# Leftover scatters of a graph kernel placed behind the next group's gathers, and the list sums' first step and pace changed

## The chip, the cores and the metric

The kernel runs on one core of one Trainium2 chip. A core has a matrix engine (TensorE, PE in the profile), a vector engine (VectorE, DVE), a scalar engine (ScalarE, ACT), a general engine (GpSimd, POOL) and a queue engine (SyncE, SP). POOL and SP issue most of the DMAs here; DMAs with an index per row (gathers and scatters) are issued by POOL. The metric is the device time of one launch in microseconds; the time before is the median of three runs.

## The reference

Four graph layers run one after the other on x of 16 x 1024 x 256 (16 graphs, 1024 nodes, 256 features) with one adjacency matrix adj of 1024 x 1024. A little over 1.5% of adj is nonzero, the diagonal included, so a row has some 17 neighbours.

```python
# layer 0: a score for each pair of nodes, wanted only where adj is not zero
pre_u = einsum('bud,dk->buk', h, W1[:d]);  pre_v = einsum('bvd,dk->bvk', h, W1[d:])
hidden = relu(pre_u[:, :, None, :] + pre_v[:, None, :, :] + b1)
S = sigmoid(einsum('buvk,ko->buvo', hidden, W2)[..., 0] + b2)
a = einsum('buv,bud->bvd', S * adj, h)
m = einsum('uv,bud->bvd', adj, h) * h
z = beta1 * h + beta2 * (a @ Wa + ba) + beta3 * (m @ Wm + bm)
# layer 1: neighbours' sum, projected
x = z + relu(einsum('ij,bjd->bid', adj, z) @ W.T + b)
# layers 2 and 3: attention with a rank-one logit and a dense bias
feats = x @ W1.T;  f = feats @ W2 + b2
coefs = softmax(leaky_relu(f[:, :, None] + f[:, None, :]) + adj)
x = coefs @ feats + bias2 + x
```

## The kernel before

**Lists in place of the dense pair tensor.** The scores of layer 0 are computed only for pairs that adj has. For each row the kernel finds up to 32 neighbours (SLOTS); the first 16 (FIRST) stand in the row's own list, the others in quads (QUAD, four slots) of extra rows, packed into 6 extra tiles of 128 rows (XT). The 16 graphs are treated in 4 groups (NGR) of 4 graphs (GB). For a group there are 8 tiles of 128 rows with 16 steps each and 6 extra tiles with 4 steps each: 152 score steps a group, 608 in all.

**A score step** (`score_steps`, L704 to L839) takes one slot of one tile for the four graphs of the group. POOL gathers 128 rows of v (`fetch`, L857, the indirect DMA at L695) into a tile z of 128 x 1024, four steps ahead (LEAD), with six z tiles. DVE adds u (L805), then takes relu times the score weights (L807), ACT sums each graph's 256 columns (four activations, L811). At a tile's last step the sigmoid is made (L820 to L824) and its 16 or 4 scatters are put on the list `waiting`; each writes the four graphs' scores of one slot to a dense array in HBM (`scatter`, L700). In the following steps one scatter is written per step, or two on odd steps while more than four wait (L786), each after that step's gather in POOL's queue. At the end of a group all that is left in `waiting` is written at once (L831 to L833) and the group is entered in `finished`. An engine takes the instructions of its queue in order, so a gather that is queued behind such a run of scatters waits for it.

**The order of the stages.** In a first part (`score_free`) PE computes the products that need no scores, for all 16 graphs. Then follow for each group: `with_edges`, which loads the dense scores (`load_gd`) and multiplies them with the projected features; and two times `pair_layers`, which takes two graphs through layer 1 (`layer_one`, that is `projected` and `neighbours`) and layers 2 and 3 (`front`, `scales`, `sums`). `sums` makes the attention weights m on DVE (L1036), and PE multiplies them.

**The interleaving is written out by hand.** Each of these stages is a generator that yields planned PE microseconds. `Side.along` counts them times a rate (RATE: 0.26 in the first part, 0.255 later) and advances the score steps by one for each whole unit. `paced` ties such an instruction to a PE product a few back, so that it doesn't run ahead. Score steps, stage work and list steps thus share the engines' queues in the order in which they were written. Before a group's `with_edges`, steps are forced until that group is in `finished` (L1303).

**The list sums.** The last group has no scores beside it. There the layer-1 neighbour sum of its second pair is split: nodes 768 to 1023 by products with adj (`neighbours`), nodes 0 to 767 (FAR = 6 tiles) by list: `by_lists` (L1139) gathers rows of y and adds them, weighted, into `msg`: 24 steps for the extra tiles, whose results are stored to part_d from SP, then 96 for the tiles' own slots, then 24 that add the extra rows. A tile's first step (k = 0, L1174) writes the tile on ACT; the other steps add on DVE (L1176, L1172). `far_ahead` places these 144 steps beside the first pair's layers, with a rate of 0.88 for the first 68 planned units (the first pair's `layer_one`) and 0.58 after that (L1293). At the end of layer one `onto` takes relu of the sums on ACT (L1116) and adds them to z on DVE (L1117); the fronts' products need that z. The second pair's stages begin with `from_lists`, which transposes msg on PE (L1193).

Of the kernel before, what the change touches and what calls it, by code (L numbers as in the profile page):

```python
# [12 lines left out]
AF = mybir.ActivationFunctionType  # L13
ALU = mybir.AluOpType
# [24 lines left out]
def after(tc, ins, others, kind, why):  # L39
    dep = mybir.DependencyInfo(kind, mybir.DependencyReason.DATA)  # L40
    for o in others:
        tc.add_manual_dep(ins.ins, o.ins.name, dep, reason=why)
# [23 lines left out]
def gnn_stack_kernel(  # L66
# [27 lines left out]
    nc = tc.nc  # L94
# [23 lines left out]
    def paced(ins, back=6):  # L118


        if recent:
            after(tc, ins, [recent[max(0, len(recent) - back)]], mybir.DependencyClass.Sync, "keeps pace")
        return ins
# [122 lines left out]
    NGR = B // GB  # L246
# [117 lines left out]
    with ExitStack() as stack:  # L364
# [126 lines left out]
        to = prep1.tile([P, NF], F32, name="to")  # L491
# [183 lines left out]
    with tc.If(listed > 0) as arm:  # L675
        with ExitStack() as stack:
# [13 lines left out]
            put = [Scatters(tc, f"scores {g}") for g in range(NGR)]  # L690
            finished = []
# [12 lines left out]
            def score_steps(pool):  # L704
# [8 lines left out]
                us, zt, ss = {}, {}, {}  # L713
# [62 lines left out]
                def unpack(got):  # L776
                    paced(nc.vector.tensor_copy(x_node, got[:, :, : 1 + QUAD]))
                    nc.vector.tensor_copy(x_a, got[:, :, 1 + QUAD : 1 + 2 * QUAD])
                    nc.vector.tensor_copy(x_at, got[:, :, 1 + 2 * QUAD : 1 + 3 * QUAD])

                moved, got, arrive = None, None, 0
                later = mybir.DependencyClass.NoSync
                for n, (g, t, k) in enumerate(todo):
                    if n + LEAD < len(todo):
                        last = fetch(us, zt, *todo[n + LEAD])
                    for _ in range(0 if n < HOLD else 2 if n % 2 and len(waiting) > 4 else 1):  # L786
                        if waiting:
                            group, *what = waiting.pop(0)
                            ins = scatter(*what)
                            group.add(ins)  # L790
                            after(tc, ins, [last], later, "behind the gather")
                    if moving:
                        group, *what = moving.pop(0)
                        ins = scatter(*what)
                        group.add(ins)
                        after(tc, ins, [last], later, "behind the gather")
                        arrive = n + 12
                    slots, _, at, av = lists(t)
                    z, u = zt.pop((g, t, k)), us[g, t]
                    if k == 0:  # L800
                        ss[t] = small.tile([P, FIRST, GB], F32, tag="s", name="s")
                    s = ss[t]
                    if k == 0 and (g, t) in follows:
                        sources(us, *follows[g, t])
                    paced(nc.vector.tensor_tensor(z, z, u, ALU.add))  # L805
                    zk = z.rearrange("p (c k) -> p c k", k=D)
                    nc.vector.scalar_tensor_tensor(  # L807
                        zk, zk, 0.0, w2r[:, None, :].to_broadcast([P, GB, D]), ALU.max, ALU.mult
                    )
                    for c in range(GB):  # L810
                        nc.scalar.activation(zk[:, c, :], zk[:, c, :], AF.Copy, accum_out=s[:, k, c : c + 1])  # L811
                    if n < NT:
                        search(others, n)
                    if n == NT:
                        places(others)
                    if n == NT + 4:
                        moved = to_extra_rows()
                    if k == slots - 1:
                        sv = s[:, :slots, :].rearrange("p s c -> p (s c)")
                        nc.scalar.activation(sv, sv, AF.Exp, bias=nb2, scale=-1.0)  # L820
                        nc.vector.tensor_scalar(sv, sv, 1.0, None, ALU.add)
                        nc.vector.reciprocal(sv, sv)
                        gt = small.tile([P, FIRST, GB], F32, tag="g", name="gt")
                        nc.vector.tensor_tensor(  # L824
                            gt[:, :slots, :], s[:, :slots, :],
                            av[:, :slots].unsqueeze(2).to_broadcast([P, slots, GB]), ALU.mult,
                        )
                        for j in range(slots):
                            waiting.append((put[g], dense[g % BUFS], at[:, j : j + 1], gt[:, j, :]))
                        if t == last_of[g]:  # L830
                            for group, *what in waiting:  # L831
                                group.add(scatter(*what))
                            waiting.clear()  # L833
                            finished.append(g)
                    if moved and not moving and n == arrive:
                        got = from_extra_rows(moved)
                    if got is not None and n == arrive + 24:
                        unpack(got)
                    yield  # L839

            def lists(t):
                if t < NT:
                    return FIRST, slot_v[:, t, :], slot_at[:, t, :], slot_a[:, t, :]
                return QUAD, x_node[:, t - NT, 1:], x_at[:, t - NT, :], x_a[:, t - NT, :]
# [294 lines left out]
            def by_lists(msg):  # L1139

                spares = [gd_pool.tile([P, QN, GB], F32, tag="gd", name="msg") for _ in range(4)]
                halves = [
                    t.rearrange("p n i -> p (n i)")[:, k * 2 * D : (k + 1) * 2 * D] for t in spares for k in range(2)
                ]
                msg.extend(halves[:FAR])
                part = halves[FAR:]
                nc.gpsimd.memset(part[0], 0.0)
                nc.sync.dma_start(part_d[XT * P :, :], part[0])

                nc.vector.tensor_scalar(to_u, to_u, float(XT * P), None, ALU.min)  # L1150
                todo = [(NT + i, k) for i in range(XT) for k in range(QUAD)]
                todo += [(t, k) for t in range(FAR) for k in range(FIRST)]
                todo += [(t, FIRST + q) for t in range(FAR) for q in range(NG)]
                got = {}

                def fetch_row(t, k):
                    z = got[t, k] = slot_pool.tile([P, GB * D], F32, tag="z", name="z")[:, : 2 * D]
                    if t < NT and k >= FIRST:
                        at = (k - FIRST) * NT + t
                        gather(z, part_d, to_u[:, at : at + 1])  # L1160
                    else:
                        gather(z, y_d, lists(t)[1][:, k : k + 1])

                for step in todo[:LEAD]:
                    fetch_row(*step)
                for n, (t, k) in enumerate(todo):
                    if n + LEAD < len(todo):
                        fetch_row(*todo[n + LEAD])
                    z = got.pop((t, k))
                    to = msg[t] if t < NT else part[t % len(part)]  # L1170
                    if t < NT and k >= FIRST:
                        paced(nc.vector.tensor_tensor(to, to, z, ALU.add))  # L1172
                    elif k == 0:
                        paced(nc.scalar.activation(to, z, AF.Copy, scale=lists(t)[3][:, k : k + 1]))  # L1174
                    else:
                        paced(nc.vector.scalar_tensor_tensor(  # L1176
                            to, z, lists(t)[3][:, k : k + 1], to, ALU.mult, ALU.add
                        ))
                    if t >= NT and k == QUAD - 1:
                        nc.sync.dma_start(part_d[(t - NT) * P : (t - NT + 1) * P, :], to)  # L1180
                    yield
# [100 lines left out]
            def far_ahead(z, main):  # L1282

                both = y_d.rearrange("(t p) (i d) -> p t i d", p=P, i=2)
                y = yield from projected(z, lambda i, ts, y: nc.sync.dma_start(both[:, ts, i, :], y))
                yield from neighbours(y, z, slice(FAR * P, N))
                gone, far = 0.0, Side(by_lists(msg))

                def slots():
                    nonlocal gone  # L1290
                    for us in main:
                        gone += us
                        yield us * (0.88 if gone < 68 else 0.58)  # L1293

                far.along(slots())
                for _ in far.steps:
                    pass
                yield 0
# [147 lines left out]
```

## Time and profile before

| | |
|---|---|
| median of three runs | 3205.61 us (3198.1 to 3207.4) |
| the profiled execution | 3224.95 us |
| its span, first to last instruction | 3223.1 us |
| scatters of scores on POOL (L700) | 512 of 1255 ns and 96 of 1174 ns |
| gathers of v on POOL (L695) | 512 of 1261 ns and 96 of 1285 ns |
| list steps on ACT (L1174) | 12 of 720 ns |
| list steps on DVE (L1176, L1172) | 108 of 751 ns, 24 of 690 ns |
| granted TensorE clock over the span | 0.99 |

How to read it: PE is the busiest engine, and a matmul takes the same time wherever it stands, so the time of a stage is its matmuls plus the pieces in which PE is idle or runs at a reduced clock. A timeline line gives start, duration, engine, source line, operation, output and input, how many instructions are merged in it, and in brackets how long the engine was idle before it and what ended that. Line numbers are those of the kernel; L126 is a helper that issues most products, L695 and L700 are helpers that issue all gathers and scatters, so that the tile names tell which is meant. A windows line gives, for a stretch of the span, its length and then the busy time of PE, of the weight loads, of DVE, ACT and POOL, each with a count, and after them the granted clock, the share of the DMA engines and GB/s.

### The profile page before, as it was taken

The page shows a single profiled execution, that of the slowest core. Times are in us where ns is not written, and L with a number is a line of the kernel's source. Part 1 is how long each engine was busy: PE and PEld are TensorE (multiplying, and loading weights), DVE is VectorE, ACT ScalarE, POOL GpSimd, SP SyncE. Part 2 cuts the span into 40 slices and gives each one's busy share as a digit, 9 for nine tenths or more (in the row PEclk, how much of TensorE's full clock was granted, in tenths as well). Part 3 has the DMA queues.
Part 4 walks back from the last instruction along what each step waited for, and adds up shares of the span by engine and source line. Part 5 has one row for each costly group of instructions (what it writes and reads, how often), then busy time and mean ns, then how long its engine had stood idle before and what let it go on. Part 6 is the DMA issues. An engine that isn't in the chain of part 4 may idle for free. (4 is left out here: it accounts for less than half of the span.)

```text
span 3223.1 us, 39246 instructions
## 1 busy us (share of the span) xinstructions
PE 3127.4 (97%) x12122; PEld 2203.7 (68%) x12122; DVE 2349.9 (73%) x3162; ACT 1955.7 (61%) x6524; POOL 1819.4 (56%) x1483
## 2 busy tenths in 40 slices
PE   8899999999999999999999999899999999998999
PEld 5444544545557668678876867777587688857888
DVE  7797767677774789789768978877798891147744
ACT  3245555666668767567977756688676774413342
POOL 1146778676764656657666665556676652076500
PEclk9999999999999999999999999999999999999999
DMA  9899898888889755756876575587657644485600
GB/s 315 292 323 322 267 288 263 265 242 249 271 284 343 211 167 150 229 158 203 300 233 171 158 212 177 161 284 239 187 151 212 181 145 145 131 256 154 156 7 28
DMA packets 281994, 687.48 MB, mean 213 GB/s; under 512 B 45280, under 2 KB 137440, under 8 KB 274608
## 3 DMA queue, kind: packets, MB, share of 16 engines
q0 software_dynamic: 128224, 387.80, 41.6%
q1 hardware_dynamic: 126112, 245.98, 22.2%
q10 hardware_dynamic: 27440, 51.13, 4.2%
q8 instruction: 97, 1.59, 0.2%
q14 instruction: 121, 0.99, 0.1%
HBM read 553.45 MB, written 131.32 MB: 212 GB/s over the span
## 5 line engine op out<-in xcount | busy, mean ns | idle before, releaser
L811 ACT ACTIVATE z<-z 128x256 f32<-128x256 f32 x2432 | 979.8, 407 | 642.3 <-DVE z L807 568.8
L805 DVE TENSOR_TENSOR z<-z,u 128x1024 f32<-128x1024 f32 x608 | 738.9, 1220 | 435.9 <-PE bank L126 291.9
L126 PE MATMUL bank<-feats,m 128*128 128x257 f32 x4096 | 923.3, 383 | 19.0 <-DVE m L1036 17.8
L695 POOL DMA_INDIRECT z<-v_d,slot_v x512 | 645.9, 1261 | 477.1 <-ACT z L811 264.1
L126 PEld LDWEIGHTS bank<-feats,m 128*128 128x128 f32 x4096 | 771.4, 191 | 138.4 <-DVE m L1036 19.8
L700 POOL DMA_INDIRECT dense_d<-gt,slot_at x512 | 642.5, 1255 | 186.8 <-issue 139.5
L807 DVE SCALAR_TENSOR_TENSOR z<-z,w2r 128x1024 f32<-128x1024 f32 x608 | 738.0, 1220 | 9.0
L126 PE MATMUL bank<-gc,hw 128*128 128x256 f32 x2048 | 456.6, 384 | 25.0 <-ACT gc L1064 17.8
L811 ACT ACTIVATION_READ_ACCUMULATOR z<-z 128x1 f32 x2432 | 463.3, 190 | 0.0
L126 PEld LDWEIGHTS bank<-gc,hw 128*128 128x128 f32 x2048 | 388.6, 192 | 92.5 <-ACT gc L1064 25.9
L126 PE MATMUL bank<-adj_sb,h 128*128 128x512 f32 x1024 | 443.0, 592 | 4.0 <-ACT st L322 2.4
L1036 DVE SCALAR_TENSOR_TENSOR m<-rho,tau,adj_sb 128x512 f32<-128x512 f32 x512 | 375.6, 744 | 72.1 <-PE bank L126 68.5
L126 PE MATMUL bank<-adjT_in,y 128*128 128x512 f32 (+1 forms) x960 | 401.2, 578 | 3.9 <-DMA adjT_in<-adjT_d 2.5
L126 PEld LDWEIGHTS bank<-adj_sb,h 128*128 128x128 f32 x1024 | 194.3, 190 | 244.2 <-issue 239.6
L126 PE MATMUL bank<-w,hT 128*128 128x512 f32 (+1 forms) x1024 | 336.2, 489 | 0.0
L126 PEld LDWEIGHTS bank<-adjT_in,y 128*128 128x128 f32 x960 | 181.9, 190 | 218.9 <-issue 204.3
L1064 ACT ACTIVATE gc<-gd 128x1024 f32<-128x1024 f32 x128 | 265.2, 2074 | 94.0 <-PE bank L126 59.1
L126 PEld LDWEIGHTS bank<-w,hT 128*128 128x128 f32 x1024 | 195.7, 192 | 143.0 <-issue 121.0
L126 PE MATMUL bank<-g_wT,z 128*128 128x257 f32 x1024 | 233.7, 383 | 8.2 <-DVE z L1117 8.2
L695 POOL DMA_INDIRECT z<-v_d,x_node x96 | 123.4, 1285 | 176.7 <-ACT z L811 115.7
L126 PEld LDWEIGHTS bank<-g_wT,z 128*128 128x128 f32 x1024 | 193.2, 191 | 39.0 <-DVE z L1117 8.9
L322 ACT ACTIVATE st<-bank 128x512 f32<-128x512 f32 x128 | 75.6, 590 | 104.3 <-PE bank L126 62.5
(161 smaller groups left out, 2403.2 us busy)
## 6 DMA issues: line engine op xcount, KB each, us to landing
gd<-dense_d SPq DMA_DIRECT2D x128, 512.0 KB
dense_d<-zero ACTq DMA_DIRECT2D x64, 512.0 KB
adjT_in<-adjT_d SPq DMA_DIRECT2D x112, 256.0 KB
h<-in_x_dram SPq DMA_DIRECT2D x19, 1024.0 KB
u_d<-st SPq DMA_DIRECT2D x64, 256.0 KB
v_d<-st SPq DMA_DIRECT2D x64, 256.0 KB
hw_d<-st SPq DMA_DIRECT2D x64, 256.0 KB
u<-u_d POOLq DMA_DIRECT2D x32, 512.0 KB
```

The costliest lines, as they stand in the source:

```text
L126: recent.append(nc.tensor.matmul(*args, **kw))
L322: nc.scalar.activation(st[:, c, :2, :], ps.rearrange("p (s k) -> p s k", s=2), AF.Copy)
L695: return nc.gpsimd.indirect_dma_start(out=dst, out_offset=None, in_=src[:], in_offset=bass.IndirectOffsetOnAxis(ap=at, axis=0), **how,)
L700: return nc.gpsimd.indirect_dma_start(out=dst[:], out_offset=bass.IndirectOffsetOnAxis(ap=at, axis=0), in_=src, in_offset=None,)
L805: paced(nc.vector.tensor_tensor(z, z, u, ALU.add))
L807: nc.vector.scalar_tensor_tensor(zk, zk, 0.0, w2r[:, None, :].to_broadcast([P, GB, D]), ALU.max, ALU.mult)
L811: nc.scalar.activation(zk[:, c, :], zk[:, c, :], AF.Copy, accum_out=s[:, k, c : c + 1])
L1036: nc.vector.scalar_tensor_tensor(m, r[:, cols], ta[:, jt : jt + 1], ea[:, jt, cols], ALU.max, ALU.mult)
L1064: paced(nc.scalar.activation(gc, gd.rearrange("p n i -> p i n"), AF.Copy), 16)
```

## The change

At a group's end the group is put on a new list, `ending`, in place of writing all its scatters. They stay in `waiting` and are written by the loop at L786 in the next group's first steps, each behind that step's gather. A helper `done` enters the group in `finished` when none of its scatters waits any more. For the last group the scatters are still written at once. In `by_lists` the first step of a tile is a multiplication on DVE instead of an activation on ACT, and in `far_ahead` the two rates become 0.80 and 0.61.

```diff
+                ending = []
+
+                def done(group):
+                    if ending and put[ending[0]] is group and all(w[0] is not group for w in waiting):
+                        finished.append(ending.pop(0))
...
                             group.add(ins)
                             after(tc, ins, [last], later, "behind the gather")
+                            done(group)
...
                         if t == last_of[g]:
-                            for group, *what in waiting:
+                            ending.append(g)
+                            while waiting and g == NGR - 1:
+                                group, *what = waiting.pop(0)
                                 group.add(scatter(*what))
-                            waiting.clear()
-                            finished.append(g)
+                                done(group)
...
                     elif k == 0:
-                        paced(nc.scalar.activation(to, z, AF.Copy, scale=lists(t)[3][:, k : k + 1]))
+                        paced(nc.vector.tensor_scalar(to, z, lists(t)[3][:, k : k + 1], None, ALU.mult))
...
-                        yield us * (0.88 if gone < 68 else 0.58)
+                        yield us * (0.8 if gone < 68 else 0.61)
```

## The prediction

> **What bounds the kernel now.** I read the page's busy line first, then the windows of 40 us over the whole span to find where TensorE (PE) stands still, then the timelines of the engines at those places, and the chain of waits last.
>
> ```profile
> PE 3127.4 (97%) x12122; PEld 2203.7 (68%) x12122; DVE 2349.9 (73%) x3162; ACT 1955.7 (61%) x6524; POOL 1819.4 (56%) x1483
> ```
>
> PE sets the time; it is idle for only 3223.1 - 3127.4 = 96 us, the start included. An edit pays only where it removes PE idle time (or keeps PE's clock up). Two pieces of that idle time lie where a group's scores end. This is POOL, then DVE, then PE at the end of group 2's scores (steps counted over all groups, so step 456):
>
> ```profile
> 2018.22 1.39 POOL L700 DMA_INDIRECT dense_d<-gt,slot_at  x1 [0.30 <-issue]
> ...
> 2042.14 0.97 POOL L700 DMA_INDIRECT dense_d<-gt,slot_at  x1 [0.30 <-issue]
> 2043.42 0.97 POOL L695 DMA_INDIRECT z<-v_d,slot_v  x1 [0.30 <-issue]
> ```
>
> ```profile
> 2048.03 1.23 DVE L805 TENSOR_TENSOR z<-z,u 128x1024 f32<-128x1024 f32 x1 [8.32 <-DMA z<-v_d,slot_v]
> ```
>
> ```profile
> 2052.43 9.74 PE L126 MATMUL bank<-feats,m 128*128 128x257 f32 x32 [8.19 <-DVE m L1036]
> ```
>
> POOL issues 16 scatters in a row, 24.9 us without a gather (from 2018.2 to 2043.1). Only the gathers fetched ahead are there to live on, so DVE meets a score step whose row isn't there, waits 8.32 us, and the products behind it in DVE's order (m, L1036) starve PE for 8.19 us. The windows show the second half of the price:
>
> ```profile
> 2040.00:2045.00 5.00, 4.24 (x22) 3.49 (x20) 0.00 (x0) 1.46 (x8) 3.78 (x5) 1.00 0.05 10
> 2045.00:2050.00 5.00, 0.00 (x0) 0.00 (x0) 1.97 (x3) 0.00 (x0) 4.09 (x4) 0.74 0.90 277
> 2050.00:2055.00 5.00, 2.57 (x6) 2.11 (x7) 4.36 (x6) 1.71 (x8) 2.29 (x3) 0.50 0.96 322
> 2055.00:2060.00 5.00, 5.00 (x18) 4.15 (x18) 3.77 (x4) 1.42 (x7) 0.18 (x1) 0.74 0.43 135
> ```
>
> The columns are PE, weight loads, DVE, ACT, POOL, then the granted clock: 0.50 after the gap, so matmuls run at half speed until about 2058. Group 1's end is the same picture (scatters from 1381.0 to 1406.0):
>
> ```profile
> 1412.64 6.19 PE L126 MATMUL bank<-feats,m 128*128 128x257 f32 x20 [3.12 <-DVE m L1036]
> ```
>
> The third place is the list sums beside the last group's first pair. The chain of waits, and PE there:
>
> ```profile
> 2884.00 19.65 issue
> 2903.67 5.42 another core or an unknown queue
> 2909.11 0.73 ACT msg L1174
> 2909.86 0.76 DVE msg L1176
> ```
>
> ```profile
> 2912.90 7.86 PE L126 MATMUL bank<-g_wT,z 128*128 128x257 f32 x24 [7.96 <-DVE z L1117]
> ```
>
> ACT sits behind one list step (L1174, k = 0 of list tile 2), DVE's list steps queue behind that, and the layer-one result z (L1116 on ACT, L1117 on DVE) queues behind those. PE needs z and loses 7.96 us, again with the clock at 0.50 afterwards.
>
> **What the Trainium skill says.** (1) "TensorE: Matmul & The Clock Gate", Part 1: after an idle window of about 3.4 us PE gets half its clock until it has been busy for such a window. The trace agrees: 0.50 after all three gaps. (2) "VectorE: DVE Perf Modes", the perf-mode tier table: an fp32 tensor_scalar in SBUF runs two elements a cycle, a two-tensor operation one. It agrees: the tensor_scalar of w by beta2 (L159, 128x512) took 481 ns, the list step of two tensors (L1176, same size) 750 ns. (3) "SBUF — State Buffer", two separate sides: such a two-port DVE operation locks GpSimd out, which then can't write DMA descriptors. No row of this trace isolates that. I use it as a bound: 0.48 us for each.
>
> **The change part by part, against the profiled execution (3224.95 us, span 3223.1).**
>
> *Scatters at a group's end.* 4 + 16 + 16 scatters of groups 0 to 2 leave the burst and go behind the next group's gathers, two on odd and one on even steps while more than four wait: 12 in eight steps, then four more, 12 steps in all. Group 3 keeps its burst (nothing is gathered after it). No instruction is added.
> - Removed at group 2's end: 8.19 us idle, and 32 matmuls in 9.74 us where 64 of the same took 14.04 us just before (0.219 each, 7.0 for 32): 2.7. Together 10.9 us.
> - Removed at group 1's end: 3.12 + 0.64 (L1219, 1419.46), and 20 matmuls in 6.19 for 4.4: 1.8. Together 5.6 us.
> - Group 0's end (four scatters, 758.7 to 763.7): PE stands at 5.00 of 5 in the windows there. 0.
> - What is late next: POOL now issues 2.5 DMAs a step while it drains. A scatter is 1255 ns, a gather 1261, and 0.30 lies between: 2.5 x 1.56 = 3.9 us. A step comes every 1/0.255 = 3.9 units of planned PE time (one sums stage is 14.8 units, 14.04 us in the trace), so POOL just keeps up, with four to six gathers of lead (some 15 us) as cover. Other tiles' ends drain by this same rule, and in the sums stages none of them shows a DVE wait for z over 1.5 us. Bounds: 0 if the lead holds, 5 us if POOL's DMAs take 1.5 + 0.3 us beside a full DVE (4.5 a step, eight steps, 0.6 late each). I take 1.5 us.
> - Does the next stage wait for the late scatters? Steps done by a point are planned units times the rate: 841.4 x 0.26 = 218.8 in the first part, less 8 searches: 210 scores. Group 0's stages (517.4 x 0.255) bring it to 342, group 1's (536.6 x 0.255) to 479. Group 1 is wanted at 342 and is complete at 304 + 12 = 316; group 2 at 479, complete at 456 + 12 = 468. The loop that forces steps never runs; the closest margin is 11 steps, some 43 us. Cost 0. The loads of dense scores on SP are issued after that and see finished scatters.
>
> Sum: -16.5 + 1.5 = -15.
>
> *First list step on DVE.* 12 activations of 0.72 us leave ACT (8.6 us), 12 tensor_scalars of about 0.48 come to DVE (5.8 us). In these windows DVE is busy 20 to 32 of 40 us, so neither is on the path by itself; what matters is that no list step stands in front of L1116 on ACT any more. If the two-port lock hits POOL each time, 12 x 0.48 = 5.8 us of POOL time, half of it in the stretch where POOL is the pacer. I take 0 on PE, since the new pace leaves room there.
>
> *The pace.* Before, 68 x 0.88 = 59.8 list steps are placed ahead of z's last part; after, 68 x 0.80 = 54.4. A list gather holds POOL 0.95 + 0.30 = 1.25 us, 0.80 a microsecond: 0.88 asks for more than POOL can issue, 0.80 about what it can. In the trace, DVE's step 53 ran at 2900.06. With steps 54 to 58 out of the way, z's four relu and add pairs (0.69 each) can run from PE's end of the stage at 2901.5 and z[0] is ready near 2903.6. PE has work of its own until 2904.9, so it doesn't wait. Removed: 7.96 idle, 24 matmuls in 7.86 for 5.2 (2.6), and the two gaps behind it in the same chain (0.33 and 0.50): 11.4 us. The stores of part_d also hold SP's queue: adjT_in loads at 2855.59 and 2860.00 went straight after such stores and PE waited 0.38 and 0.58. At the slower pace a store falls one load later: another 1.0 at most. In the profiled execution I make this -12.
>
> How much of it is in an ordinary run? The profiled execution is 19 us longer than the median of the three runs shown (3205.61), and 5.42 us of this stall ends by nothing that the profile can name: its gather had landed at 2903.65, its matmuls were recorded done. If an ordinary run lacks those 5.4 us, PE waits about 2.5, too short to lose the clock, and 0.8 + 0.7 for the small gaps: 4 us. The median decides, so I take -4 there (bounds 0 and -12).
>
> *The tail.* 213.9 planned units give 144.5 steps before and 143.4 after; there are 144. So one list step is placed after the pair's last work. It is a 0.69 us add, and PE first transposes four other list tiles (16 transposes, 1.75 us). 0 to 1.3; I take 0.5.
>
> Sum against the profile: -15 - 12 + 0.5 = -26.5, 3198. Against the median: -15 - 4 + 0.5 = -18.5, **3187 us**.
>
> **The rivals.**
> - *Forecast (0.53): both stalls go, 3187.* For it: the burst, the late gather, the wait and the half clock stand in one line. Against: DVE is at 38.5 of 40 us in the sums stages, so it has little to catch up with.
> - *POOL's pace takes the place of the burst (0.20).* The stall is spread, PE gets half of it back later: -8 - 3 = -11, 3195. For it: POOL's 3.9 us a step against 3.9 available. Against: 15 us of lead, and the other tiles' ends.
> - *It doesn't show (0.15).* If POOL runs faster outside the profile (a burst of 17 us instead of 25 would end before the lead is gone) there was no stall to remove; the list stall is the profile's: 3203.
> - *Slower (0.12): the list sums bound the last group.* The second part now holds 89 steps where it held 84.6, in the 150 us from 2912 to 3062: 1.69 us a step. POOL needs 1.21 + 0.30 = 1.51 beside a busy DVE. If a step really costs 2.0 (two-port lock, contention for DMAs), the lists end 89 x 0.31 = 28 us late and PE waits at the transposes: 3187 + 28 = 3215. It costs from 1.69 a step on and turns the sign at 1.69 + 18.5/89 = 1.90. Against: gathers in that stretch mostly wait about 0.5 us for DVE, that is, they are paced, not pacing.
>
> **How the numbers follow.** 0.3% is 9.6 us, about what a measurement of this kernel can tell from no change. The forecast's own range is 3175 (both stalls whole, 30 us) to 3195; with the rivals 3174 to 3206 leaves some 2 in 10 out. Faster by over 0.3%: the forecast nearly whole, three quarters of the second case, little of the third: 0.69. Within: 0.19. Slower: 0.12.
>
> **What would show it.** Right: after each group's last score step POOL alternates gathers and scatters; no DVE wait over 3 us for z there, no clock of 0.50; PE runs through from the last adjT_in product to the fronts in group 3, L1116 with no list step before it on ACT. Wrong: a DVE wait for z of several microseconds some ten steps into the next group; a wait of the dense loads on scatters; PE idle before the transposes of msg (L1193); or the profile improving by over 20 us while the median doesn't move.

## The result and the profile after

The changed kernel takes 3181.4 us, the median of six runs (3169.6 to 3185.6), against 3205.8 us for six runs of the kernel before on the same chip: a ratio of 0.9921, 95% interval [0.9902, 0.9941], 24.4 us less. The profiled execution takes 3181.81 us with a span of 3180.1; that of before had 3223.1. So the profiles differ by 43 us and the medians by 24: the profiled execution of before lay 19 us above its median, that of after lies on its median. The forecast was 3187.

The busy line of the page after (line numbers after the change are 7 or 8 higher than before):

```profile
PE 3117.1 (98%) x12122; PEld 2198.4 (69%) x12122; DVE 2354.2 (74%) x3174; ACT 1946.7 (61%) x6512; POOL 1823.1 (57%) x1483
```

The number of matmuls is the same and PE is still the bound, but it is idle for 3180.1 - 3117.1 = 63 us instead of 96, and its busy time fell by 10 us as well: the clock granted to it, averaged over the span, is 0.994 in place of 0.990. DVE has 12 instructions more and ACT 12 fewer.

POOL at the end of group 2's scores, the place where before had 16 scatters in a row (timeline: start, duration, engine, line, operation, output and input, idle before it):

```profile
2002.52 0.96 POOL L695 DMA_INDIRECT z<-v_d,slot_v  x1 [1.04 <-ACT feats L988]
2003.79 1.38 POOL L700 DMA_INDIRECT dense_d<-gt,slot_at  x1 [0.30 <-issue]
...
2008.55 0.97 POOL L700 DMA_INDIRECT dense_d<-gt,slot_at  x1 [0.30 <-DMA z<-v_d,slot_v]
2009.83 0.97 POOL L695 DMA_INDIRECT z<-v_d,slot_v  x1 [0.30 <-issue]
2011.11 1.36 POOL L700 DMA_INDIRECT dense_d<-gt,slot_at  x1 [0.30 <-issue]
2012.77 1.48 POOL L700 DMA_INDIRECT dense_d<-gt,slot_at  x1 [0.31 <-issue]
2014.56 1.49 POOL L695 DMA_INDIRECT z<-v_d,slot_v  x1 [0.30 <-issue]
```

A gather now comes after four scatters, then after one or two. POOL issues without a pause until the last of the 16 at 2044.07. What DVE waited for over this stretch (1990 to 2060 us; total, times, longest), and two of the 5 us windows (PE, weight loads, DVE, ACT, POOL, granted clock):

```profile
DVE z L812 <- PE bank L126: 2.4, 4, 0.8
DVE m L1044 <- PE bank L126: 0.8, 1, 0.8
```

```profile
2035.00:2040.00 5.00, 5.00 (x27) 4.37 (x26) 5.00 (x11) 4.49 (x20) 4.09 (x4) 1.00 0.58 193
2040.00:2045.00 5.00, 5.00 (x25) 4.37 (x24) 4.71 (x6) 4.02 (x17) 4.09 (x4) 1.00 0.77 218
```

DVE waits for no gather at all (before: 8.32 us for one), PE is busy all the time and the clock stays at 1.00. At the end of group 1 it is the same. In the last group, PE and DVE before the fronts:

```profile
2831.70 38.03 PE L126 MATMUL bank<-adjT_in,y 128*128 128x512 f32 x88 [1.28 <-DMA adjT_in<-adjT_d]
2869.57 8.85 PE L126 MATMUL bank<-g_wT,z 128*128 128x257 f32 x40
```

```profile
2868.62 1.28 DVE L1125 TENSOR_TENSOR z<-z,r 128x512 f32<-128x512 f32 x2
2870.49 1.28 DVE L1125 TENSOR_TENSOR z<-z,r 128x512 f32<-128x512 f32 x2
```

z is ready while PE still has products of its own, so PE goes from the last adjT_in product to the fronts (g_wT) without the 7.96 us. One wait for an adjT_in load, 1.28 us, is left.

To compare runs, three stages are measured from the start times of products in each kernel's PE timeline. A: group 1's second pair, from its first g_wT product to the next group's first gc product. B: the same for group 2. C: the last group's first pair with the list sums, from its first 512-wide adjT_in product to the first transpose of msg.

| profile | ratio of times [95%] | A, us | B, us | C, us |
|---|---|---|---|---|
| before | 1 | 159.2 | 164.7 | 220.4 |
| after | 0.9921 [0.9902, 0.9941] | 152.7 | 152.5 | 206.8 |
| scatters_only | 0.9932 [0.9913, 0.9950] | 152.8 | 153.9 | 221.4 |
| list_only | 0.9977 [0.9962, 0.9992] | 159.4 | 164.8 | 214.6 |
| dve_only | 0.9996 [0.9985, 1.0007] | 159.3 | 164.7 | 224.0 |
| pace_only | 0.9970 [0.9958, 0.9982] | 159.4 | 164.6 | 213.1 |
| before_again | - | 159.2 | 162.9 | 222.5 |
| after_again | 0.9906 [0.9891, 0.9920] | 152.7 | 153.9 | 215.7 |
| slower_lists | 0.9903 [0.9888, 0.9917] | 152.8 | 153.9 | 205.3 |
| eight_at_once | 0.9939 [0.9926, 0.9952] | 152.8 | 158.6 | 213.9 |
| stores_later | 0.9921 [0.9901, 0.9941] | 152.8 | 152.5 | 206.2 |
| slower_stores_later | 0.9905 [0.9889, 0.9921] | 152.8 | 152.5 | 205.0 |
| all_late | one run | 152.8 | 152.5 | 238.3 |
| list_again | 0.9974 [0.9964, 0.9985] | 159.1 | 164.9 | 215.7 |

From before to after A, B and C fall by 6.5, 12.2 and 13.6 us, 32 of the 43 us. The other 11 us lie in stages in which the change was to do nothing (4.6 of it before the first group's dense products), so they are put down to the two executions and not to the change. C holds more than the stall before the fronts: PE's waits within the adjT_in stage (0 to 4.5 us by profile) and those between the fronts and the transposes are in it too.

### The profile page after: what moved, and what is told of

Read it like the earlier page. It is cut to its first block, busy times and chain, and to the rows that moved or that the text cites. A ratio compares the mean times of both kernels' runs of the same rounds, so it can differ in the third digit from the quotient of the medians.

```text
span 3180.1 us, 39242 instructions
## 1 busy us (share of the span) xinstructions
PE 3117.1 (98%) x12122; PEld 2198.4 (69%) x12122; DVE 2354.2 (74%) x3174; ACT 1946.7 (61%) x6512; POOL 1823.1 (57%) x1483
## 4 chain that ended last, share of the span: by engine, by line
PE 78%; DVE 8%; DMA 6%; ACT 4%; issue 2%; POOL 1%; SPq 0%; ACTq 0%; DVEq 0%; POOLq 0%
PE bank L126 75%; DMA z<-v_d,slot_v 2%; DVE z L812 2%; ACT z L818 2%; DVE z L814 2%; ACT gc L1072 1%; DVE slot_a L440 1%; DMA gd<-dense_d 1%; PE bank L1227 1%; DVE left L442 1%; DVE m L1044 1%; PE bank L1010 1%; POOL z L695 1%; PE bank L1251 1%; POOL dense_d L700 1%
## 5 line engine op out<-in xcount | busy, mean ns | idle before, releaser
L126 PEld LDWEIGHTS bank<-adjT_in,y 128*128 128x128 f32 x960 | 182.0, 190 | 215.7 <-issue 201.2
```

The source lines that it names most:

```text
L126: recent.append(nc.tensor.matmul(*args, **kw))
```

## The experiments

The sets fell on different chips. The kernel before takes 3206 us beside the stores and all_late kernels, as in the first comparison, and 3236 to 3238 us beside all others. So times are compared within a set only, as ratios to the kernel before.

**Taking the change apart.** Four kernels have one part each.

scatters_only, the new end of a group with list steps and pace as before:

```diff
-                        paced(nc.vector.tensor_scalar(to, z, lists(t)[3][:, k : k + 1], None, ALU.mult))
+                        paced(nc.scalar.activation(to, z, AF.Copy, scale=lists(t)[3][:, k : k + 1]))
...
-                        yield us * (0.8 if gone < 68 else 0.61)
+                        yield us * (0.88 if gone < 68 else 0.58)
```

> Only the first part of the change: scatters left over at the end of groups 0 to 2 behind the next group's gathers; list steps and pace as before. My theory (both bursts stalled PE in every execution): 3205.8 minus 15 to 19, so 3187 to 3191 (ratio 0.994 to 0.995); in the profile the stages after the adjT_in products of group 1's and group 2's second pair are 6.4 and 12.2 us shorter than before (159.2 and 164.7 us), and the list stall before the fronts of the last group (7.96 us in the profile of before) is still there. Rival, POOL's pace takes the burst's place: 3195 or more, and a wait of DVE for z of several us in group 3's first steps. Rival, the bursts stall only under the profiler: within 4 us of before.

Measured: 3214.5 against 3236.0 us, -22 us by the ratio (interval -28 to -16). Stages A and B lose 6.4 and 10.8 us, C stays. DVE waits for no gather at either place. The list stall is there, as PE's timeline of this kernel shows:

```profile
2894.88 3.64 PE L126 MATMUL bank<-g_wT,z 128*128 128x257 f32 x16
2902.45 2.94 PE L126 MATMUL bank<-g_wT,z 128*128 128x257 f32 x6 [3.93 <-DVE z L1125]
```

Both rivals fall: the bursts stalled ordinary executions too, and no wait for a gather came in their place. The ratio lies a little below the 0.994 to 0.995 that was expected; 17 of the 22 us are seen in A and B.

list_only, the new list step and pace with the scatters written at once as before:

```diff
-                            while waiting and g == NGR - 1:
+                            while waiting:
```

> Only the second part of the change: first list step of a tile on DVE and the pace 0.80 / 0.61; the scatters at a group's end written at once as before. My theory, as in the prediction: 4 us less than before in the median (ratio 0.9987), although the profiled stage from the list pair's adjT_in products to the transposes of msg is some 13.6 us shorter than in the profile of before. Rival, the list stall is there whole in every execution: 12 to 14 us less (ratio 0.996). Rival, list sums now bound the last group: slower than before, with PE idle before the transposes of msg.

Measured: 3227.6 against 3236.0, -7.4 us (-12.3 to -2.6). A and B are as before (DVE again waits 8.3 us for one gather, PE 8.16); C is 5.8 us shorter than before, not the 13.6 that was expected of it. The time falls between theory (-4) and rival (-12 to -14), and some of the stall is left (3.23 us before the fronts).

dve_only, only the engine of the step; against list_only:

```diff
-                        yield us * (0.8 if gone < 68 else 0.61)
+                        yield us * (0.88 if gone < 68 else 0.58)
```

> Only the engine of a tile's first list step: on DVE instead of ACT, pace 0.88 / 0.58 as before. My theory (the pace does the work: DVE's queue still has list steps in front of z's last adds, and these wait for POOL's gathers): the same time as before within 3 us, and PE still idle 4 to 8 us before the fronts of the last group. Rival (the ACT step in front of L1116 is what stalls, so moving it is enough): the stall is under 1 us and the time that of the second part whole. Rival (DVE's two-port form holds POOL up): 3 to 6 us slower than before.

Measured: 3233.5, ratio 0.9996, no difference that can be told. PE waits 4.81 us before the fronts. ACT and DVE there:

```profile
2903.70 0.69 ACT L1124 ACTIVATE r<-bank,l1b 128x512 f32<-128x512 f32 x1 [24.20 <-PE bank L126]
...
2906.27 0.69 ACT L1124 ACTIVATE r<-bank,l1b 128x512 f32<-128x512 f32 x1 [0.17 <-issue]
```

```profile
2907.54 0.75 DVE L1184 SCALAR_TENSOR_TENSOR msg<-z,slot_a,msg 128x512 f32<-128x512 f32 x1 [0.74 <-DMA z<-y_d,slot_v]
2909.06 0.49 DVE L1182 TENSOR_SCALAR msg<-z,slot_a 128x512 f32<-128x512 f32 x1 [0.77 <-DMA z<-y_d,slot_v]
2910.57 0.75 DVE L1184 SCALAR_TENSOR_TENSOR msg<-z,slot_a,msg 128x512 f32<-128x512 f32 x1 [1.02 <-DMA z<-y_d,slot_v]
...
2913.78 1.89 DVE L1125 TENSOR_TENSOR z<-z,r 128x512 f32<-128x512 f32 x3
```

The four relus are done by 2907, with nothing in front of them on ACT. DVE comes to z's adds only at 2913.78, since it first has list steps to do, one every 1.5 us, each of which waits for its own gather. So this stall needs no list step on ACT: the pace of 0.88 has put steps in front of z that POOL can't serve in time.

pace_only, only the pace; against the kernel before:

```diff
-                        yield us * (0.88 if gone < 68 else 0.58)
+                        yield us * (0.8 if gone < 68 else 0.61)
```

> Only the pace, 0.80 / 0.61; a tile's first list step stays on ACT. My theory: this alone removes the list stall (54.4 list steps ahead of z's last part instead of 59.8, and the ACT step of list tile 2 is the 57th), so it gives what the second part whole gives, within 2 us; no PE wait above 1 us before the fronts of the last group. Rival (the engine of the step is what matters): the stall of several us is still there and the time that of before.

Measured: 3227.1, -9.7 us (-13.6 to -5.8), as much as both list edits together, within what the intervals allow. PE before the fronts:

```profile
2907.64 7.55 PE L126 MATMUL bank<-g_wT,z 128*128 128x257 f32 x34
2916.30 1.14 PE L126 MATMUL bank<-g_wT,z 128*128 128x257 f32 x4 [1.11 <-issue]
```

So the pace does the work of the second part; the engine of the step adds nothing that can be told. The wait of 1.11 us is a little above the bound of the expectation.

**The whole change and the size of a burst.** after_again is the changed kernel once more, with no further edit.

> The whole change once more, beside the kernels of this set. My theory (the two parts add up, and the scatters carry the most): 0.991 to 0.992 of before on any chip, 24 to 29 us less; the stages after the adjT_in products of group 1's and group 2's second pair stay at 152.5 to 154 us, with no DVE wait for z above 3 us. Where PE's releases come late (a relu L1124 several us after the last product of its bank was recorded, with ACT idle), some of the list stall is left: 1 to 4 us before the fronts of the last group. Rival (the two parts share a gain): 18 to 22 us less.

Measured: 3206.2 against 3238.2, ratio 0.9906, -30 us (-35 to -26): the two parts add up, 22 + 7. But C is 215.7 here and 206.8 in the first profile of the same kernel: 5.72 us of the list stall are back. ACT, DVE and PE there:

```profile
2893.66 0.69 ACT L1124 ACTIVATE r<-bank,l1b 128x512 f32<-128x512 f32 x1 [32.96 <-remote]
```

```profile
2888.03 2.33 DVE L1184 SCALAR_TENSOR_TENSOR msg<-z,slot_a,msg 128x512 f32<-128x512 f32 x3 [4.29 <-PE bank L126]
2894.38 0.69 DVE L1125 TENSOR_TENSOR z<-z,r 128x512 f32<-128x512 f32 x1 [4.02 <-ACT r L1124]
```

```profile
2885.76 3.64 PE L126 MATMUL bank<-g_wT,z 128*128 128x257 f32 x16
2895.12 1.23 PE L126 MATMUL bank<-g_wT,z 128*128 128x257 f32 x2 [5.72 <-DVE z L1125]
```

PE's last adjT_in product is recorded before 2886, and nothing stands in front of the relu on ACT (idle for 33 us), yet the relu starts at 2893.66 ("remote": the view can't name what ended the wait). In the first profile of after the first relu started at 2867.20, before the last product of the stage had ended. The semaphore events in the trace tell what it waited for: one semaphore of DVE, last raised at 2888.79, and one of PE, raised at 2893.64. So the release of PE's results came some 8 us late here, and no list step on ACT explains that.

eight_at_once writes all but the last eight at a group's end:

```diff
-                            while waiting and g == NGR - 1:
+                            while len(waiting) > (0 if g == NGR - 1 else 8):
```

> The whole change, but at the end of groups 0 to 2 all scatters beyond eight are written at once and only the last eight are left to go behind the next group's gathers. Eight of 16 in a row hold POOL 8 x 1.56 = 12.5 us. My theory (the stall is what is left of the burst after the gathers fetched ahead are used up, a lead of about 15 us): no stall at all, the same time as the change within 3 us, both stages at 152.5 to 154 us. Rival (each scatter written at once costs its share): half of the gain of that part is lost, 8 to 11 us more than the change, DVE waits of about 4 us for z.

Measured: ratio 0.9939, some 11 us above the change (3218.7 and 3206.2 in the same set). So the expected time did not come; time and DVE wait lie near what the rival said, and the stages must decide. A is 152.8, all of the gain; B is 158.6, 4.7 above the change. POOL, DVE and PE at the end of group 2:

```profile
2026.33 1.38 POOL L700 DMA_INDIRECT dense_d<-gt,slot_at  x1 [0.30 <-issue]
...
2043.96 1.56 POOL L700 DMA_INDIRECT dense_d<-gt,slot_at  x1 [0.30 <-issue]
2045.83 1.03 POOL L695 DMA_INDIRECT z<-v_d,slot_v  x1 [0.30 <-issue]
```

```profile
2050.88 1.23 DVE L812 TENSOR_TENSOR z<-z,u 128x1024 f32<-128x1024 f32 x1 [3.06 <-DMA z<-v_d,slot_v]
```

```profile
2055.27 8.68 PE L126 MATMUL bank<-feats,m 128*128 128x257 f32 x32 [2.92 <-DVE m L1044]
```

The expectation had a burst of 8 and 12.5 us, and that was its mistake. In POOL's queue 12 stand in a row, since four of those left over precede the next gather (as in the profile of after), so the burst lasts from 2026.33 to 2045.83, 19.5 us. That makes the run a measurement of the lead. With 16 in a row (2018.22 to 2043.42, 25.2 us) DVE waited 8.32, so the lead is 16.9 us; 19.5 us should then leave a wait of 2.6, and 3.06 was measured. At group 1's end the lead is 25.35 - 7.0 = 18.3 us; the burst of 12 there lasts 17.1 (1390.17 to 1407.31), and DVE waits for no gather. A share of the gain lost for each scatter would have shown in A too, and A lost nothing. So the stall is what the burst has beyond the lead. Of the 11 us only 4.7 are seen in B; the rest isn't explained by a stage that this kernel alters (of the 17.7 us between the two profiles, 15.7 lie before the first group's dense products), and the two intervals would let the 11 be 6 us smaller or larger.

before_again is the kernel before, unaltered, for a second profile.

> The kernel before once more, for a second profile of it. My theory: both stalls at the groups' ends are there again with the same size within 0.5 us (DVE waits of 7.0 and 8.3 us for z, PE 3.1 and 8.2), since they come from the order of POOL's queue; the list stall before the fronts of the last group varies from one execution to the next, anywhere from 2 to 8 us, since part of it is a late release. Rival (the list stall is as fixed as the others): 7.5 to 8.5 us again.

Measured: DVE waits 7.0 and 7.9 us for z at the two group ends, PE 3.16 and 7.79: as in the first profile within 0.5 us. The list stall came as 5.76 and 2.35 us in place of 7.96; C is 222.5 and was 220.4. ACT there, in before_again and then in the first profile of before:

```profile
2915.74 0.72 ACT L1174 ACTIVATE msg<-z,slot_a 128x512 f32<-128x512 f32 x1 [20.36 <-PE bank L126]
2921.39 0.69 ACT L1116 ACTIVATE r<-bank,l1b 128x512 f32<-128x512 f32 x1 [4.93 <-remote]
```

```profile
2909.11 0.72 ACT L1174 ACTIVATE msg<-z,slot_a 128x512 f32<-128x512 f32 x1 [25.11 <-remote]
2910.57 2.52 ACT L1116 ACTIVATE r<-bank,l1b 128x512 f32<-128x512 f32 x4 [0.74 <-remote]
```

In before_again the list step on ACT is over at 2916.46, and ACT then idles 4.93 us before the first relu. The semaphore events name PE in both profiles: it raised the semaphore at 2921.37 and the relu started at 2921.39; in before it raised it at 2909.08 (list step, 2909.11; its gather had landed long before) and at 2910.55 (relu, 2910.57). PE's last adjT_in products are recorded as done by 2913.63 and 2901.46. So in both profiles of the kernel before it was the late release of PE, as in after_again, that held z up, and not the list step in front of the relu. All four profiles with the old pace have C at 220.4 to 224.0; in scatters_only and dve_only, where the first relu came 2.4 us after and 2.5 us before the end of the last product, the stall of 3.93 and 4.81 us is made by list steps that wait for gathers.

**The pace of the list sums.** slower_lists, the whole change with a lower pace at first:

```diff
-                        yield us * (0.8 if gone < 68 else 0.61)
+                        yield us * (0.72 if gone < 68 else 0.65)
```

> The whole change with the list pace 0.72 / 0.65 in place of 0.80 / 0.61: 49.0 list steps ahead of z's last part, 95 in the rest. My theory (0.80 is already what POOL can issue, what is left of the stall is PE's late release and no list step): the same as the change within 4 us, the stage up to the fronts unchanged or 1 to 2 us shorter, and the rest at 1.58 us a step still above POOL's 1.51, so no PE wait before the transposes of msg. Rival (list steps in front of z's last adds still cost): 4 to 7 us less than the change. Rival (list sums bound the last group, a step of over 1.6 us): PE waits before the transposes of msg, 5 to 20 us more than the change.

Measured: 3204.4 against 3206.2 for the change in the same set, no difference in time. In the profile C is 205.3, with no stall at all. ACT and PE before the fronts:

```profile
2882.41 0.69 ACT L1124 ACTIVATE r<-bank,l1b 128x512 f32<-128x512 f32 x1 [23.04 <-PE bank L126]
```

```profile
2829.52 55.42 PE L126 MATMUL bank<-adjT_in,y 128*128 128x512 f32 x128
2884.78 7.55 PE L126 MATMUL bank<-g_wT,z 128*128 128x257 f32 x34
```

One wait of 0.60 us has come after the transposes of msg (for z), so the lists end just in time.

stores_later issues each store of part_d three list steps later:

```diff
-                        nc.sync.dma_start(part_d[(t - NT) * P : (t - NT + 1) * P, :], to)
+                        done_parts.append((n + 3, t, to))
+                    if done_parts and done_parts[0][0] == n:
+                        _, x, part_x = done_parts.pop(0)
+                        nc.sync.dma_start(part_d[(x - NT) * P : (x - NT + 1) * P, :], part_x)
```

> The whole change, and each store of part_d is issued three list steps later, so that SP finds its list step done and doesn't hold the adjT_in loads behind it. My theory (the stores are a small cause beside the pace): PE's waits for adjT_in beside the list sums (0.6 to 1.3 us each with the change) go, 1 to 3 us of time, and some of the stall before the fronts stays in those executions in which PE's releases come late. Rival (the late loads are what makes the stall before the fronts): it is gone, 5 to 9 us less than the change, so a ratio near 0.988 where the change has 0.9906. Rival (nothing): the same as the change.

Measured: ratio 0.9921, as the change in its own first comparison. One wait for an adjT_in load is left in the stage, 0.63 us where the change had 1.28. The stores are worth less than can be measured.

slower_stores_later has both of these edits, the lower pace and the later stores:

> As the kernel with the later stores, with the list pace 0.72 / 0.65. My theory (changed after the run with this pace alone, whose profile had no stall left before the fronts): the list pair's two stages together come to 205 to 207 us in the profile, PE waits at most 1 us before the transposes of msg, and the time is 3 to 8 us below that of the kernel with the later stores alone. Rival (0.80 is enough, the rest is chance between executions): equal within 2 us. Rival (list sums bound): a wait of several us before the transposes of msg.

Measured: 3177.8 us, ratio 0.9905, against 3183.6 for stores_later in the same set; C 205.0, and 0.60 us of PE wait behind the transposes of msg. It is the fastest kernel of its set, 30 us (25 to 36) below before. That it beats the change by 6 us isn't shown, since the intervals overlap; what is shown in two profiles of two is that the stall before the fronts is gone at 0.72.

all_late, the whole change with no list step placed ahead of z's last part:

```diff
-                        yield us * (0.8 if gone < 68 else 0.61)
+                        yield us * (0.0 if gone < 68 else 0.99)
```

> The whole change with a list pace of 0 / 0.99: no list step ahead of z's last part, all 144 in the rest, 1.03 us a step against POOL's 1.25 (its bare issue) to 1.51 (beside a busy DVE). My theory for the slower rival's price: PE runs through to the fronts (the stage of the adjT_in products at 54.9 to 55.5 us), and then waits before the transposes of msg for the steps that POOL couldn't issue, 144 x 1.25 to 144 x 1.51 against some 150 us: 30 to 67 us; the run is slower than the change by 20 to 60 us. If a step costs 2.0 as the slower rival had it, 288 us are needed and PE waits 138 us.

Measured in one run: 3237.2 us, 54 us above stores_later in the same set. The groups of the tile msg on DVE (form, count, shortest, median and longest, first and last start):

```profile
L1184 DVE SCALAR_TENSOR_TENSOR msg<-z,slot_a,msg x90: 730/746/809, 2905.0 to 3042.6; 128x512 f32<-128x512 f32 x90
L1180 DVE TENSOR_TENSOR msg<-msg,z x24: 676/692/743, 3040.5 to 3074.9; 128x512 f32<-128x512 f32 x24
L1182 DVE TENSOR_SCALAR msg<-z,x_a x6: 478/483/490, 2873.7 to 2898.6; 128x512 f32<-128x512 f32 x6
```

144 steps run from 2873.7 to 3074.9: 1.40 us a step, between POOL's 1.25 and 1.51 as expected, and not 2.0. The adjT_in stage takes 54.9 us. The stretch from the fronts to the first transpose of msg then grows by 33 us. Not as expected, this isn't one wait ahead of the transposes: PE's waits are spread over the stretch (the longest is 6.23 us for m, which on DVE stands behind list steps, one of which waited 3.50 us for its gather). Within the transposes 18 us more are lost (21.0 us instead of 3.0).

list_again repeats list_only, with no further edit:

> The second part alone once more (first list step on DVE, pace 0.80 / 0.61; scatters as before), on another chip if it comes to one. My theory (the stall before the fronts is there in ordinary executions of before): 7 to 10 us less than before, ratio 0.997 to 0.998, both on a chip on which before takes 3236 and on one on which it takes 3206. Rival, as the prediction had it (an ordinary execution has only 4 us of it): ratio 0.9985 to 0.999. In the profile the stages after the adjT_in products of group 1's and 2's second pair are at 159.2 and 163 to 165 us again.

Measured: 3228.5 against 3237.2, ratio 0.9974, -8.4 us (-11.7 to -4.9). The set came to a chip on which before takes 3237 again, so the second part alone was never timed on one with 3206. The 4 us of the prediction lie just outside the interval (inside that of list_only). In this profile PE doesn't wait before the fronts at all; C is 215.7 because of 3.8 us of waits within the adjT_in stage and one of 4.39 us for m behind the fronts.

## Why the prediction was right, and which term was too small

- *Stall at group 2's end, -10.9.* Right: B fell by 12.2 us in the profile of the change and by 10.8 in scatters_only.
- *Stall at group 1's end, -5.6.* Right, and a little small: A fell by 6.4 to 6.5 us in every kernel that defers the scatters. The gap of 0.89 at 1435.62 that went too was not in the sum. The 1.8 us of half clock in it are not a fixed loss: in before_again PE waited 3.16 us there, the clock stayed at 1.00, PE then waited 2.10 us for val in place of 0.64, and A is 159.2 all the same.
- *Cost of the drain, 1.5, bounds 0 and 5.* It is 0: A is 152.7 us, B 152.5 and 153.9, and no DVE wait for a gather is left. POOL issues 26 DMAs from 2002.5 to 2044.1, 1.66 us from one to the next where the sum had 1.56, and the lead of 15 us (measured: 16.9 and 18.3) carries it. Its order was not quite "two on odd and one on even steps": four scatters come in a row first, 7.3 us between two gathers, which is still inside the lead.
- *Finished in time, no forced steps: 0.* In the profile of after no wait of the dense products appears that before didn't have (the next group's stage took 116.2 and 118.9 us, before 116.2 and 120.4). In scatters_only and after_again the second of them took 126.3 and 126.0, with a wait of 3.4 and 3.7 us for ACT's copy of the scores. The loads of these scores were issued from 36 us after the last scatter on in both, as in after, so nothing points to the scatters; the cause is open.
- *First list step on DVE: 0 on PE.* Right: dve_only, 0.9996. The instruction takes 486 ns, 0.48 in the sum, and ACT's busy time fell by 9.0 us for 8.6. The bound taken from the Trainium skill ("SBUF — State Buffer", two separate sides: a two-port DVE operation locks GpSimd out) shows nowhere: dve_only is no slower, and the 12 gathers of y that run at the same time as one of these steps take 1048 ns on average in after, against 1083 ns before, when the step was on ACT.
- *The pace: -12 in the profile, -4 in an ordinary run.* That the pace is what counts was right: pace_only has the whole gain. The term for the median was mis-sized: list_only, list_again and pace_only measured -7.4, -8.4 and -9.7. The text had "If an ordinary run lacks those 5.4 us, PE waits about 2.5", and took the unnamed 5.42 us for something of the one execution. It was PE's late release, and it came again in before_again. The text also had z behind one list step on ACT; in both profiles of before the relu started only when PE released it. What it described, list steps ahead of z that wait for gathers, is what scatters_only and dve_only show. So the -12 for the profile is right in part by luck: C fell by 13.6 us in a pair of profiles of which the first had the late release and the second had not, and by 4.7 to 6.8 us from the two profiles of before to after_again, which had it again. Without a late release the stall is 3.93 and 4.81 us in the two profiles at the old pace, and 0 to 1.11 us in the five at 0.80 (after, list_again, pace_only, eight_at_once, stores_later).
- *The 0.80 itself, "about what it can".* A little too fast: the 1.25 us count POOL's shortest gather (0.95); the 120 gathers of y in before take 1.075 us on average, which with 0.30 makes 1.38, and all_late needed 1.40 us a step, 0.71 a microsecond. The stall is gone in both profiles at 0.72.
- *The tail, 0.5.* Nothing: the transposes take 3.03 us before and after.
- *The rivals.* POOL's pace in place of the burst: no. Doesn't show: no. Slower, the lists as bound at 2.0 us a step: a step costs 1.40 (all_late) with the change leaving 1.69; the turn at 1.90 was far.

With measured terms the sum is -18.7 us for A and B in the profile of the change (-17.2 in scatters_only), 0 for the drain and -7.4 to -9.7 for the pace: -25 to -28 us, where -24.4 was measured, with an interval of -31 to -19. The forecast of -18.5 stands at the edge of that interval. The pace's term was some 4 us too small, the bursts' 1 to 2 us, and the drain's 1.5 didn't come; the single microseconds are below what the times can tell, and the -7.4 to -9.7 are from chips on which before takes 3236 us or more.

The warning sign "the profile improving by over 20 us while the median doesn't move" came half: the profile improved by 43 us, the median by 24. The 19 us that the profiled execution of before lay above its median were in the comparison of profiles from the start; stage by stage 11 us of them can be told apart, since they fall in stages in which the change was to do nothing.

## What to carry to other kernels

A run of slow DMA issues ahead of a prefetch queue cost its length minus the lead here, and nothing where it was shorter than the lead: work out the lead in time from a burst and the wait behind it, test it with a second length, and spread only what exceeds it. Where two streams share an issuing engine, ask for no more than its issue rate (here 1.40 us a step); a pace above that puts steps that can't be served in front of the work that the bound engine needs. When one profiled execution is slower than its median, compare it stage by stage, and don't write off a stall that is in the changed stage as an accident of that execution before a second profile shows it so. And ask of each wait what ended it: an instruction that stands in front in the queue may itself have waited for the same release.

## What was not expected of the hardware

- PE's results can be released many microseconds after the products are recorded. In after_again the relu on ACT started at 2893.66 with ACT idle and the products recorded as done by 2886; in the first profile of the same kernel the first relu came 2.4 us before the next stage's first product. The same lateness stands in before, before_again and list_only (relu at 2912.65, fronts' first product at 2907.31): in 2 of 4 profiles at the old pace, in 2 of 7 at 0.80, and in none of the three with 0.72 or no list steps there. Where in PE those microseconds go, or whether the products end later than they are recorded, and whether a lower rate of gathers is the reason, stays open.
- The same kernel takes 3206, 3236, 3238 or 3237 us by set and chip, 1% apart, as much as the change is worth. The change gives 0.9921 on the one and 0.9906 on the other, so its ratio carries over where its time doesn't.
- How far one profile can be trusted depends on the stage: A is 152.7 to 152.8 us in all eight profiles that defer group 1's scatters, while C, in which gathers, loads and PE wait for each other, is 206.8 and 215.7 for the same kernel.
